# PSUM banks given out by number, the mixed key tile weighted in one pass, row sums over fewer slabs, shift copies on ScalarE

## The chip, the cores and the metric

The kernel runs on one core of a Trainium2 chip. The metric is device time in microseconds of one execution; the number for a kernel is the median of several executions.

## The reference

The input is x (4 sequences of 512 rows, 512 features) and a context of 1601 rows for each sequence, all fp32. Two parts follow each other.

The first is cross attention with 16 heads of 32 features on the layer norm of x. The first 257 context rows are an image part and the other 1344 a text part. Each has its own key and value weights; queries and keys are normalised by their root mean square and scaled. The queries attend to the text part and, in a softmax of its own, to the image part; the two results are added, projected and added to x.

```
q = rms_norm(linear(ln(x), q_w, q_b), norm_q_w)
k, v         = rms_norm(linear(ctx[:, 257:], k_w, k_b), norm_k_w), linear(ctx[:, 257:], v_w, v_b)
k_img, v_img = the same of ctx[:, :257] with the image weights
x = x + linear(attention(q, k, v) + attention(q, k_img, v_img), o_w, o_b)
```

The second is a mixture of experts on the layer norm of the new x (2048 tokens): a router picks 4 of 32 experts for each token out of its three best of 8 groups, each expert takes at most 80 tokens, and a shared gated layer is added.

## The kernel before

The work is put in order by hand: each engine executes its instructions in the order in which the Python program emits them, and waits are set by the use of tiles. A tile's buffer is written again once all uses of its last holder are done.

*Attention.* The outer loop runs over the 4 sequences `b`. For each, the keys of all heads are computed in four blocks (`keys`, L513 on; block 3 is the image part), with other work put between the chunks by the table `side` (L555) and the list after it. Then an inner loop runs over `c` = 0 to 3. One (b, c) is called a unit here: a group of 4 heads, 32 features each, so that a head `g` stands on partitions 32g to 32g+31. There are 16 units.

A unit walks over 13 key tiles `t` of 128 keys (`NKT`). The keys are laid out text first, so tile 10 (`MIX`) holds 64 text keys on the lower and 64 image keys on the upper partitions, and tile 12 has 65 keys. In each step t stand:

- `wave` (L312), only for c < 3: scores of queries against 512 keys for the *next* unit, four matmuls of 32 contraction rows side by side, and their maxima on VectorE (L336, L338, L331).
- `exps` (L364): for each of the 4 heads a bf16 matmul that puts in the negated maxima (L370, the shift, from `mT`), a matmul of keys by queries (L373) and the exponential on ScalarE (L374) into `pT` of that tile.
- `consume(t - 2)`: `weighted` (L376) multiplies the values with the exponentials of two steps ago into the bank `po`, four matmuls of 32 output columns each side by side (L379). Tile 10 ends the text sum and begins the image sum: its text half is weighted, `po` is copied out by ScalarE (`taken`, L604), a new `po` is taken, and its image half is weighted behind `exps` of that step.
- `added` (L381): the exponentials of the text tiles 0 to 9 are summed in `acc`, two adds of 128x1024 a tile, on GpSimd for c < 3 and on VectorE for c = 3 (L388).
- one value tile of the next unit (`value_tile`, L284), or for c = 3 a piece of the next sequence's queries, and other pieces, by `fill`.

The last two tiles and the row sums are put off: `pending` (L673) holds consume(11), consume(12) and `end`, which the next unit takes out at t = 0 (two) and t = 1 (L631, L646). Behind c = 3 the first is taken at once and the others in the next sequence's `side[(0, 0)]`, or, behind the last unit, in the loop over the first two shared projections at the end (L910). `end` calls `summed` (L390), which reduces four slabs over the partitions by matmuls with 0 and 1 (`sums`): `acc` and tiles 10, 11 and 12. `normalize` (L408) then sends the sums through DRAM to turn them about (den, reciprocal, `rb`), scales the two outputs on GpSimd (L423, L424) and adds them on VectorE into `aoT` (L425); `Later` counts the steps between these.

Before a unit, `split` (L340) forms the shifts of its maxima on VectorE as three bf16 terms, and `shifts` (L355) turns them by four transposes and copies the result to `mT` on VectorE (L361).

*Buffers.* The eight PSUM banks are a ring of 7 for all (`psum`) and one for `po`:

```
ring = pool("ring", 7, space=PSUM)
pso = pool("pso", 1, space=PSUM)
```

`pT` has 5 buffers, which also take the weights of the next sequence (wk, wki, wo, loaded by SP's queue) and the first tile of the shared layer (`first_xT`, L681). `po_s`, `den` and `sq_q` share 4 buffers.

*After attention* come the shared layer, with routing on VectorE between its projections, and the 32 experts, whose weights stream in.

Of the kernel before, what the change touches and what calls it, by code (L numbers as in the profile page):

```python
# [103 lines left out]
def body(ctx, tc, a, ident, mhalf, logits, x1_d, xw_d, xnT_d, den_d, rec_d, out):  # L104
# [10 lines left out]
    ring = pool("ring", 7, space=PSUM)  # L115
    pso = pool("pso", 1, space=PSUM)
    later = Later()

    def psum(dt=F32):

        shape = [P, 512] if dt is F32 else [P, NQ, P]
        return ring.tile(shape, dt, name="ps", tag="ring")
# [232 lines left out]
    def shifts(part):  # L355

        ps = psum(BF16)
        for qt in range(NQ):
            nc.tensor.transpose(ps[:, qt, :], part[:, qt, :], ident_b)
        mT = st.tile([P, L], BF16, name="mT", tag="mT", bufs=2)  # L360
        nc.vector.tensor_copy(mT, ps.rearrange("p t q -> p (t q)"))  # L361
        return mT
# [13 lines left out]
    def weighted(po, v, t, rows, pT, start, stop):  # L376
        for g in range(NG4):
            r = HD * g
            nc.tensor.matmul(po[r:r + HD, :], lhsT=v[rows, t, r:r + HD], rhs=pT[rows, g, :], start=start, stop=stop)  # L379

    def added(acc, pTs, t, idle):  # L381

        if t < 1 or t >= MIX:
            return
        for half in range(2):
            h = slice(2 * half, 2 * half + 2)
            engine = nc.vector if idle else nc.gpsimd
            engine.tensor_tensor(acc[:, h, :], pTs[0][:, h, :] if t == 1 else acc[:, h, :], pTs[t][:, h, :], ALU.add)  # L388

    def summed(acc, pTs):  # L390

        ps = psum()
        slabs = [(acc, 0)] + [(pTs[t], t) for t in range(MIX, NKT)]
        for j, (p, t) in enumerate(slabs):
            n = key_rows(t)
            for g in range(NG4):
                nc.tensor.matmul(
                    ps[g * HD:(g + 1) * HD, :],
                    lhsT=sums[:n, kind(t)].rearrange("p a b -> p (a b)"),
                    rhs=p[:n, g, :],  # L400
# [92 lines left out]
    for b in range(B):  # L493
# [52 lines left out]
        def due():  # L546
# [9 lines left out]
            (0, 0): [due, due, N("q")],  # L556
# [30 lines left out]
        for c in range(NC):  # L587
# [10 lines left out]
            def consume(t, c=c, v=v, pTs=pTs, outs=outs, pos=pos):  # L598

                n = key_rows(t)  # L600
                if t == 0:
                    pos.append(pso.tile([P, L], F32, name="po"))

                def taken():  # L604
                    o = held("po_s")
                    nc.scalar.copy(o, pos[-1])  # L606
                    outs.append(o)

                def text():
                    weighted(pos[0], v, t, slice(0, HALF), pTs[t], False, True)  # L610
                    taken()
                    pos.append(pso.tile([P, L], F32, name="po"))

                def image():
                    weighted(pos[1], v, t, slice(HALF, P), pTs[t], True, False)

                def all_():
                    weighted(pos[-1], v, t, slice(0, n), pTs[t], t == 0, t == NKT - 1)
                    if t == NKT - 1:
                        taken()  # L620

                return (text, image) if t == MIX else (all_, lambda: None)

            for t in range(NKT):
# [4 lines left out]
                if t == 0 and c:  # L629
                    mT = shifts(part)  # L630
                if t < 2 and pending:  # L631
                    pending.pop(0)()
                if t == 1:
                    g["acc"] = kv.tile([P, NG4, L], F32, name="acc")
                    if more:
                        v_next = kv.tile([P, NKT, P], F32, name="v", bufs=2)
                        fill = values(v_next, c + 1, cTs, ws)
                    elif b + 1 < B:
                        fill = work
                behind = consume(t - 2) if t > 1 else [lambda: None] * 2  # L640
                behind[0]()
                exps(c, t, qT, kT, mT, pT)
                if t:
                    added(g["acc"], pTs, t - 1, not more)
                behind[1]()
                if t == 0 and pending:  # L646
                    pending.pop(0)()
                if c == 0 and t < 3:
# [21 lines left out]
            def end(i=b * NC + c, c=c, aoT=aoT, outs=outs, acc=g["acc"], pTs=pTs):  # L670
# [349 lines left out]
```

## Time and profile before

| | |
|---|---|
| median of 3 runs | 1824.26 us (1822.17 to 1825.31) |
| profiled execution: time, span of its instructions | 1826.59 us, 1824.9 us |
| granted TensorE clock, mean | 0.987 |
| TensorE (PE) busy | 1737.6 us, 95% |
| VectorE (DVE), ScalarE (ACT), GpSimd (POOL) busy | 960.6, 614.8, 773.6 us |
| weighting matmuls L379, 1792 records | 238.7 us busy |
| exponentials L374, 832 | 429.4 us, 602 ns each |
| adds on GpSimd L388, 216 | 505.8 us, 2384 and 2353 ns each |
| adds on VectorE L388, 72 | 88.2 us, 1278 and 1221 ns each |
| matmuls of the row sums L397, 512 records | 64.0 us busy |

An fp32 matmul shows as two records, one for each pass; a bf16 matmul as one. Records of matmuls that run side by side overlap, and the end of a record is modelled, so the time that a group takes is read from its start to the next group's start. Times in the timelines are microseconds from the start of the span.

### The profile page before, as it was taken

What the parts mean: (1) busy time and instruction counts of PE and PEld (TensorE: products, weight loads), DVE (VectorE), ACT (ScalarE), POOL (GpSimd) and SP (SyncE); (2) the same over time, 40 slices, a digit from 0 to 9 for tenths busy, and PEclk for the clock granted to TensorE, in tenths of its full rate; (3) what the DMA queues carried; (4) which work ended last, traced back from release to release, by engine and by line L of the source; (5) the groups of instructions that cost most, each with busy time, mean ns of one, the idle gap of its engine ahead of it and who ended that gap; (6) DMA issues with size and microseconds to landing.
All of it is one profiled execution on the core that took longest, in us unless ns stands there. A gap on an engine that the chain in (4) does not pass through costs nothing. (4 is left out here: it accounts for less than half of the span.)

```text
span 1824.9 us, 29627 instructions
## 1 busy us (share of the span) xinstructions
PE 1737.6 (95%) x11985; PEld 906.5 (50%) x11985; DVE 960.6 (53%) x1881; ACT 614.8 (34%) x1324; POOL 773.6 (42%) x540
## 2 busy tenths in 40 slices
PE   4999999999999999999999999999999999999896
PEld 1564444446644444565444445644442454477664
DVE  2485557628555556475556547655465567611110
ACT  1124444621344446114444551144446110011111
POOL 1319558122468552326477323284591110123332
PEclk9999999999999999999999999999999999999898
DMA  6000000040100102120001030200012173279894
GB/s 217 1 1 1 19 5 28 22 146 29 65 1 20 31 2 105 62 68 27 11 10 31 14 143 18 98 13 14 2 36 82 65 252 104 65 250 296 267 294 118
DMA packets 68024, 138.41 MB, mean 76 GB/s; under 512 B 16048, under 2 KB 28464, under 8 KB 65584
## 3 DMA queue, kind: packets, MB, share of 16 engines
q1 hardware_dynamic: 62768, 125.70, 20.2%
q0 software_dynamic: 5120, 10.82, 2.9%
q8 instruction: 95, 1.56, 0.4%
q14 instruction: 41, 0.34, 0.1%
HBM read 113.68 MB, written 22.81 MB: 75 GB/s over the span
## 5 line engine op out<-in xcount | busy, mean ns | idle before, releaser
L374 ACT ACTIVATE pT<-ps 128x512 f32<-128x512 f32 (+1 forms) x832 | 429.4, 602 | 418.8 <-PE ps L373 407.8
L336 DVE TENSOR_REDUCE mx<-ps 128x1 f32<-128x512 f32 (+1 forms) x576 | 330.9, 616 | 294.6 <-PE ps L322 294.5
L388 POOL TENSOR_TENSOR acc<-acc,pT 128x1024 f32<-128x1024 f32 x192 | 449.8, 2384 | 10.6 <-ACT pT L374 10.6
L379 PE MATMUL po<-pT,v 128*32 128x512 f32 (+2 forms) x1792 | 238.7, 604 | 0.4 <-ACT po_s L606 0.4
L292 PEld LDWEIGHTS ps<-v_w,cT 128*128 128x128 f32 (+1 forms) x1408 | 170.5, 189 | 92.6 <-DVE mx L336 48.5
L373 PE MATMUL ps<-qT,kT 32*128 32x512 f32 (+1 forms) x1664 | 215.7, 589 | 0.0
L322 PE MATMUL ps<-kT,qT 32*128 32x512 f32 (+1 forms) x1536 | 202.5, 553 | 0.0
L292 PE MATMUL ps<-v_w,cT 128*128 128x128 f32 (+1 forms) x1408 | 196.8, 286 | 0.0
L232 PE MATMUL ps<-cT,wk 128*128 128x512 f32 (+1 forms) x384 | 153.1, 545 | 0.0
L310 DVE TENSOR_REDUCE mx<-ps 128x1 f32<-128x512 f32 (+2 forms) x256 | 128.3, 565 | 7.8 <-PE ps L307 7.8
L388 POOL TENSOR_TENSOR acc<-pT 128x1024 f32<-128x1024 f32 x24 | 56.0, 2353 | 168.0 <-ACT pT L374 168.0
L370 PEld LDWEIGHTS <-pick 32*128 32x128 bf16 (+1 forms) x832 | 22.2, 91 | 185.8 <-issue 162.5
L370 PE MATMUL ps<-mT,pick 32*128 32x512 bf16 (+1 forms) x832 | 87.8, 385 | 21.9 <-DVE mT L361 12.5
L894 POOL DMA_INDIRECT out<-y,tok x32 | 45.4, 1419 | 143.2 <-DMA out<-y,tok 85.0
L232 PEld LDWEIGHTS ps<-cT,wk 128*128 128x128 f32 x384 | 69.9, 190 | 69.4 <-issue 58.8
L379 PEld LDWEIGHTS po<-pT,v 128*32 128x32 f32 (+2 forms) x1792 | 35.4, 107 | 133.3 <-issue 112.7
L239 POOL TENSOR_TENSOR sq_k<-sq_k,sq 128x512 f32<-128x512 f32 (+2 forms) x48 | 49.5, 1031 | 121.7 <-ACT sq L236 121.7
L884 DVE TENSOR_TENSOR ehT<-ehT,ps 128x160 f32<-128x160 f32 x32 | 10.3, 321 | 164.3 <-ACT ehT L883 164.3
L300 ACT COPY v<-ps 128x128 f32<-128x128 f32 (+1 forms) x208 | 58.4, 289 | 108.3 <-PE ps L292 107.7
L322 PEld LDWEIGHTS ps<-kT,qT 32*128 32x128 f32 x1536 | 79.3, 185 | 28.8 <-issue 11.6
L239 POOL TENSOR_TENSOR sq_q<-sq_q,sq 128x128 f32<-128x128 f32 (+1 forms) x39 | 23.3, 605 | 162.5 <-ACT sq L236 162.4
L373 PEld LDWEIGHTS ps<-qT,kT 32*128 32x128 f32 (+1 forms) x1664 | 80.8, 180 | 16.8 <-issue 12.5
(173 smaller groups left out, 2142.3 us busy)
## 6 DMA issues: line engine op xcount, KB each, us to landing
W_gate<-in_W_gate SPq DMA_DIRECT2D x32, 512.0 KB, 5.8
W_up<-in_W_up SPq DMA_DIRECT2D x32, 512.0 KB, 7.0
W_down<-in_W_down SPq DMA_DIRECT2D x32, 512.0 KB, 4.9
xt<-in_x SPq DMA_DIRECT2D x32, 256.0 KB, 2.6
cT<-in_ctxT SPq DMA_DIRECT2D x8, 1024.0 KB, 9.0
rb<-rec_d SPq DMA_DIRECT2D x64, 128.0 KB, 2.7
wk<-in_k_w SPq DMA_DIRECT2D x4, 1024.0 KB
wki<-in_k_img_w SPq DMA_DIRECT2D x4, 1024.0 KB, 9.2
```

Of the source, the lines that this page charges most:

```text
L232: nc.tensor.matmul(ps[:, :n], lhsT=wt[:, k, c * P:(c + 1) * P], rhs=xT[:, k, to], start=k == 0, stop=k == NC - 1)
L239: nc.gpsimd.tensor_tensor(sq[:, to], sq[:, to], s, ALU.add)
L292: nc.tensor.matmul(ps[lo:hi, :], lhsT=cTs[bl][:, k, at:at + hi - lo], rhs=ws[bl == NB - 1][:, k, c * P:(c + 1) * P], start=k == 0, stop=k ...
L300: nc.scalar.copy(v[:n, t, :], ps[:n])
L310: nc.vector.tensor_reduce(mx[:, qt, g, bl:bl + 1], ps[:, :n], AX.X, ALU.max, negate=True)
L322: nc.tensor.matmul(ps[:, j * n:(j + 1) * n], lhsT=qT[r:r + HD, c, q * P:(q + 1) * P], rhs=kT[r:r + HD, c, k0:k0 + n], start=True, stop=True,)
L336: nc.vector.tensor_reduce(mx[:, qt, g, i:i + 1], ps[:, :m], AX.X, ALU.max, negate=True)
L370: nc.tensor.matmul(ps[:n], lhsT=pick[r:r + HD, kind(t), :n], rhs=mT[r:r + HD, :], start=True, stop=False)
L373: nc.tensor.matmul(ps[:n], lhsT=kT[r:r + HD, c, t * P:t * P + n], rhs=qT[r:r + HD, c, :], start=False, stop=True)
L374: nc.scalar.activation(pT[:n, g, :], ps[:n], AF.Exp)
L379: nc.tensor.matmul(po[r:r + HD, :], lhsT=v[rows, t, r:r + HD], rhs=pT[rows, g, :], start=start, stop=stop)
L388: engine.tensor_tensor(acc[:, h, :], pTs[0][:, h, :] if t == 1 else acc[:, h, :], pTs[t][:, h, :], ALU.add)
```

## The change

The two PSUM pools become one of eight single buffers, named by bank number. A list gives the banks out in turn; `kept` takes one out of the list for `po`, and `taken` puts it back after the copy. At tile 10 both halves are now weighted in one loop over the heads, text and image alternating, each into its own bank, ahead of `exps` of that step.

In c < 3 tile 12 is added to tile 11 (its 65 partitions) by GpSimd after consume(11), so that `summed` has three slabs: `acc`, tile 11 and tile 10. In c = 3 VectorE also adds the text half of tile 10 to `acc` and its image half to tile 11, so that there are two. `end` is taken at t = 2 instead of t = 1, `acc` is begun at t = 2 after it, and the first value tile of t = 1 is put ahead of `exps`. For c > 0 the shift copy is done by ScalarE. At the start of a sequence the pending tasks are taken one step apart, and likewise at the first two shared projections.

```diff
-    ring = pool("ring", 7, space=PSUM)
-    pso = pool("pso", 1, space=PSUM)
+    ring = pool("ring", 1, space=PSUM)
+    banks = list(range(8))
...
-        return ring.tile(shape, dt, name="ps", tag="ring")
+        banks.append(banks.pop(0))
+        return ring.tile(shape, dt, name="ps", tag=f"bank{banks[-1]}")
+
+    def kept():
+
+        n = banks.pop(0)
+        return ring.tile([P, 512], F32, name="po", tag=f"bank{n}"), n
...
-    def shifts(part):
+    def shifts(part, copy=nc.vector.tensor_copy):
...
-        nc.vector.tensor_copy(mT, ps.rearrange("p t q -> p (t q)"))
+        copy(mT, ps.rearrange("p t q -> p (t q)"))
...
-    def weighted(po, v, t, rows, pT, start, stop):
+    def weighted(v, t, pT, *to):
+
         for g in range(NG4):
             r = HD * g
-            nc.tensor.matmul(po[r:r + HD, :], lhsT=v[rows, t, r:r + HD], rhs=pT[rows, g, :], start=start, stop=stop)
-
-    def added(acc, pTs, t, idle):
-
-        if t < 1 or t >= MIX:
-            return
+            for po, rows, start, stop in to:
+                nc.tensor.matmul(
+                    po[r:r + HD, :], lhsT=v[rows, t, r:r + HD], rhs=pT[rows, g, :], start=start, stop=stop
+                )
+
+    def added(to, pT, rows, idle):
+
         for half in range(2):
             h = slice(2 * half, 2 * half + 2)
-            engine = nc.vector if idle else nc.gpsimd
-            engine.tensor_tensor(acc[:, h, :], pTs[0][:, h, :] if t == 1 else acc[:, h, :], pTs[t][:, h, :], ALU.add)
+            (nc.vector if idle else nc.gpsimd).tensor_tensor(to[rows, h, :], to[rows, h, :], pT[rows, h, :], ALU.add)
+
+    def begun(pTs, idle):
+
+        acc = kv.tile([P, NG4, L], F32, name="acc")
+        for half in range(2):
+            h = slice(2 * half, 2 * half + 2)
+            (nc.vector if idle else nc.gpsimd).tensor_tensor(acc[:, h, :], pTs[0][:, h, :], pTs[1][:, h, :], ALU.add)
+        return acc
...
-            (0, 0): [due, due, N("q")],
+            (0, 0): [due, N("q")],
+            (0, 1): [due],
...
+            def taken(pos=pos, outs=outs):
+                po, n = pos.pop(0)
+                o = held("po_s")
+                nc.scalar.copy(o, po)
+                banks.append(n)
+                outs.append(o)
+
+            def consume(t, v=v, pTs=pTs, pos=pos, taken=taken):
+
+                if t in (0, MIX):
+                    pos.append(kept())
+                if t == MIX:
+                    weighted(
+                        v, t, pTs[t], (pos[0][0], slice(0, HALF), False, True), (pos[1][0], slice(HALF, P), True, False)
+                    )
+                else:
+                    weighted(v, t, pTs[t], (pos[0][0], slice(0, key_rows(t)), t == 0, t == NKT - 1))
+                if t in (MIX, NKT - 1):
                     taken()
...
                 if t == 0 and c:
-                    mT = shifts(part)
-                if t < 2 and pending:
+                    mT = shifts(part, nc.scalar.copy)
+                if t in (0, 2) and pending:
                     pending.pop(0)()
                 if t == 1:
-                    g["acc"] = kv.tile([P, NG4, L], F32, name="acc")
                     if more:
                         v_next = kv.tile([P, NKT, P], F32, name="v", bufs=2)
                         fill = values(v_next, c + 1, cTs, ws)
+                        fill[0]()
+                        done = 1
...
-                behind = consume(t - 2) if t > 1 else [lambda: None] * 2
-                behind[0]()
+                if t > 1:
+                    consume(t - 2)
                 exps(c, t, qT, kT, mT, pT)
-                if t:
-                    added(g["acc"], pTs, t - 1, not more)
-                behind[1]()
                 if t == 0 and pending:
                     pending.pop(0)()
+                if t == 2:
+                    g["acc"] = begun(pTs, not more)
+                elif 2 < t <= MIX:
+                    added(g["acc"], pTs[t - 1], slice(0, P), not more)
+                elif t == NKT - 1 and not more:
+                    added(g["acc"], pTs[MIX], slice(0, HALF), True)
...
+            def image(consume=consume, pTs=pTs, idle=not more):
+
+                consume(NKT - 2)
+                added(pTs[NKT - 2], pTs[NKT - 1], slice(0, key_rows(NKT - 1)), idle)
+                if idle:
+                    added(pTs[NKT - 2], pTs[MIX], slice(HALF, P), idle)
+
+            def end(i=b * NC + c, c=c, aoT=aoT, outs=outs, acc=g["acc"], pTs=pTs, idle=not more):
+                slabs = [(acc, 0), (pTs[NKT - 2], 2)] + ([] if idle else [(pTs[MIX], 1)])
+                normalize(i, c, aoT, *outs, summed(slabs))
+
+            pending += [image, partial(consume, NKT - 1), end]
...
         u()
-        while pending:
+        if pending:
             pending.pop(0)()
         later.step()
```

More of the change, by code (lines that the diff above doesn't have):

```diff
@@ L374, in exps, with summed @@
             nc.scalar.activation(pT[:n, g, :], ps[:n], AF.Exp)
-    def weighted(po, v, t, rows, pT, start, stop):
+    def weighted(v, t, pT, *to):
         for g in range(NG4):
             r = HD * g
-            nc.tensor.matmul(po[r:r + HD, :], lhsT=v[rows, t, r:r + HD], rhs=pT[rows, g, :], start=start, stop=stop)
-    def added(acc, pTs, t, idle):
-        if t < 1 or t >= MIX:
-            return
+            for po, rows, start, stop in to:
[3 more added lines that the diff above has]
+    def added(to, pT, rows, idle):
         for half in range(2):
             h = slice(2 * half, 2 * half + 2)
-            engine = nc.vector if idle else nc.gpsimd
-            engine.tensor_tensor(acc[:, h, :], pTs[0][:, h, :] if t == 1 else acc[:, h, :], pTs[t][:, h, :], ALU.add)
-    def summed(acc, pTs):
+            (nc.vector if idle else nc.gpsimd).tensor_tensor(to[rows, h, :], to[rows, h, :], pT[rows, h, :], ALU.add)
[5 more added lines that the diff above has]
+        return acc
+    def summed(slabs):
         ps = psum()
-        slabs = [(acc, 0)] + [(pTs[t], t) for t in range(MIX, NKT)]
-        for j, (p, t) in enumerate(slabs):
-            n = key_rows(t)
+        for j, (p, k) in enumerate(slabs):
             for g in range(NG4):
@@ L398, in summed @@
                     ps[g * HD:(g + 1) * HD, :],
-                    lhsT=sums[:n, kind(t)].rearrange("p a b -> p (a b)"),
-                    rhs=p[:n, g, :],
+                    lhsT=sums[:, k].rearrange("p a b -> p (a b)"),
+                    rhs=p[:, g, :],
                     start=j == 0,
@@ L596, in body @@
             pTs, outs, pos, g = [], [], [], {}
[L598 to L610, printed above, removed]
-                    taken()
[L612 to L622, printed above, removed]
+            def taken(pos=pos, outs=outs):
[14 more added lines that the diff above has]
+                if t in (MIX, NKT - 1):
+                    taken()
             for t in range(NKT):
@@ L668, in body @@
                         turn[t // 3][1]()
-            def end(i=b * NC + c, c=c, aoT=aoT, outs=outs, acc=g["acc"], pTs=pTs):
-                normalize(i, c, aoT, outs[0], outs[1], summed(acc, pTs))
-            pending += [lambda consume=consume, t=t: consume(t)[0]() for t in (NKT - 2, NKT - 1)] + [end]
+            def image(consume=consume, pTs=pTs, idle=not more):
[7 more added lines that the diff above has]
+            pending += [image, partial(consume, NKT - 1), end]
             if more:
```

## The prediction, made before the changed kernel had run

> **What bounds the kernel now.** I read the page's engine rows and slices first, then the timeline of TensorE across a boundary of two head groups, then the list of its waits in the same windows.
>
> ```profile
> PE 1737.6 (95%) x11985; PEld 906.5 (50%) x11985; DVE 960.6 (53%) x1881; ACT 614.8 (34%) x1324; POOL 773.6 (42%) x540
> PE   4999999999999999999999999999999999999896
> ```
>
> TensorE is full in all slices but the first and those of the experts at the end. Attention runs from about 130 to 1415 us, and there nearly every matmul removed is time removed. The chain of waits holds only the tail's scatter, so I work from timelines. The end of c=0 and the start of c=1 in sequence b=1 (start, length, engine, line; in brackets the idle time before):
>
> ```profile
> 534.86 1.06 PE L379 MATMUL po<-pT,v 64*32 64x512 f32 x8
> 535.85 0.41 PE L370 MATMUL ps<-mT,pick 32*65 32x512 bf16 x4
> 536.09 1.03 PE L373 MATMUL ps<-qT,kT 32*65 32x512 f32 x8
> 537.05 1.06 PE L379 MATMUL po<-pT,v 64*32 64x512 f32 x8
> 538.04 1.09 PE L292 MATMUL ps<-v_img_w,cT 128*65 128x128 f32 x8
> 539.06 1.14 PE L322 MATMUL ps<-kT,qT 32*128 32x512 f32 x8
> 540.13 0.40 PE L359 MATMUL ps<-ident_b,parts 128*128 128x128 bf16 x4
> 540.46 1.06 PE L379 MATMUL po<-pT,v 128*32 128x512 f32 x8
> 543.09 0.40 PE L370 MATMUL ps<-mT,pick 32*128 32x512 bf16 x4 [1.56 <-DVE mT L361]
> ```
>
> Rows overlap at their ends, so starts are the clock. The two 64-row groups of the mixed tile (534.86, 537.05) take 0.99 us each to the next start. The second follows the scores with no gap, so the wait for the one `po` bank, 13.5 us in the list of waits, lies under other work. At 543.09 TensorE stood still for 1.56 us: the shift copy waits on VectorE behind four maxima.
>
> ```profile
> 546.34 1.06 PE L397 MATMUL ps<-acc,sums 128*32 128x512 f32 x8
> 547.22 2.76 PE L397 MATMUL ps<-pT,sums 128*32 128x512 f32 x24
> 549.91 0.40 PE L370 MATMUL ps<-mT,pick 32*128 32x512 bf16 x4
> ```
>
> Four slabs of row sums: 547.22 to 549.91 is three, about 0.865 us each (0.43 us a pass, two passes). And one stall in c=2:
>
> ```profile
> 635.56 2.46 DVE L425 SCALAR_TENSOR_TENSOR aoT<-po_s,v_b 128x512 f32<-128x512 f32 x1
> 637.94 2.57 DVE L221 TENSOR_SCALAR xl<-xt,mv,rstd 128x512 f32<-128x512 f32 x1
> 641.16 0.37 PE L370 MATMUL ps<-mT,pick 32*128 32x512 bf16 x1 [2.25 <-DVE mx L336]
> ```
>
> Two VectorE operations that take 0.74 and 0.44 us elsewhere take 2.5 each, back to back, while GpSimd adds; the maxima then come late and banks are not free. The step from the shift matmuls at 638.53 to the next at 647.48 is 8.95 us against 5.01 for its like (624.46 to 629.47), partly because matmuls after the gap are slower: 3.94 us lost. It occurs three times (gaps near 288, 639 and 990 us).
>
> **What the skill says.** "TensorE: Matmul & The Clock Gate", Packing small matmuls, says that tiles of different row and column groups run together and that both kinds compose. The trace agrees for four row tiles (L373) and four column tiles (L379), 7 ns apart in start; eight of 64x32 it doesn't show. "SBUF — State Buffer", Who interferes with whom, says that VectorE with two SBUF inputs, or in a two-port mode, and GpSimd block each other, and tensor_reduce never does: the 2.5 us rows agree, and the maxima keep their 0.6 us. The clock page's account that idleness throttles TensorE agrees with the values group after that gap, 1.91 us instead of 1.16.
>
> **The change, part by part** (16 units: 4 sequences of c=0..3).
>
> *Mixed tile.* The image group moves beside the text group. If eight tiles run as four do, one 0.99 us is saved per unit. But in c=0 and 1 (8 units) the next wave then comes 0.99 us sooner, and its fourth bank waits for the second exp of tile 12: exps start 1.12 us after the scores and take 0.52 each, so it is free at 2.2 against a wave at 2.0; cost 0.24. Leaves 8 x 0.75 = 6.0. At the ends of c=3 for b<3, 3 x 0.99 = 3.0. At c=2's end the gain meets the shift copy, next.
>
> *Shift copy to ScalarE*, 12 copies. This form isn't in the trace; the nearest rows are ScalarE's fp32 copies of 128x512, 0.59 to 0.62 us, and VectorE's own copy, 0.42. I take 0.6; up to 1.0 would hide in c=1 and 2. In c=1 and 2 ScalarE is through with tile 12 before the transposes end, and the copy hides under consume(11), 1.0 us: 8 x 1.56 = 12.5. In c=3 there is no wave; VectorE was free and nothing waited. Now the copy queues behind tile 12's exps, the copy of xl and the value copy: these end 3.8 us after the scores began (674.85), so it ends at 4.4, where TensorE wants it at 3.65. That costs 0.8 of c=2's 0.99 (leaves 0.2, x4 with b=3, where no xl copy stands but TensorE is sooner too). Total for the mixed tile, this charged: 6.0 + 3.0 + 0.8 = 9.8.
>
> *Row sums.* c<3 drops one slab, c=3 two: 12 x 0.865 + 4 x 1.73 = 17.3. The one at the start of b=3's c=3 counts below, so 16.4. For it GpSimd adds tile 12 onto tile 11, 2 x 2.36 us (L388's row) in t=0, after consume(11) and tile 12's exps. Behind it queue only inv_sqrt and the next `acc`. The sums now stand in t=2: between lie exps, consume(12), a wave, two values, exps and a wave, about 8 us, so it hides; in c=3 about 5 us, and its slab comes after `acc`'s 0.87. Without that cover up to 4.7 us per unit would show. Per unit GpSimd rises from about 45 to 50 us, under some 62. In c=3 VectorE makes six adds of 1.2 us at the end instead, under keys (3.6 us a chunk) and consume(12); ready about 5 us after consume(11), needed after 9. The weights loaded into these buffers (wo on SP's queue) wait for the last add rather than for the sums, about as late as now.
>
> *`end` one step later.* It moves den's two DMAs, rec's store and rb's four loads on SP, the reciprocal, GpSimd's two scalings and aoT by a step; in c=2 the SP ones fall behind an x load of 0.37 us. rb is issued by 560.4 and used at 567.0, so there is slack. In c=2 aoT now follows t=6 and xl stays at t=5: two blocked operations no longer meet. One alone makes the maxima at most about 1 us late, with 0.5 slack. Unknown in size: 0 if they still meet, 11.8 (3 x 3.94) if not; single blocked ones leave no gap now, so I take 10. The first value matmul takes the place of the sums in t=1: no cost, as none is added.
>
> *Banks by number.* po waits cost nothing now, so nothing is gained; six are left for a moment at the mixed tile, but the bank taken held the third exp of tile 11, done 0.6 us earlier. Zero; up to 0.5 x 16 = 8 lost if not.
>
> *Last unit* (b=3, c=3). VectorE's adds bound it: the xT load is issued when its buffer's add is done.
>
> ```profile
> 1403.68 0.61 SPq L681 DMA_DIRECT2D xT<-xnT_d  x1
> 1409.73 2.80 PE L226 MATMUL ps<-xT,shared_gate 128*128 128x512 f32 x4 [3.02 <-DMA xT<-xnT_d]
> ```
>
> Here the matmuls saved are lost in that wait. But exps(1) comes before the sums, so VectorE begins at about 1379.0 rather than 1381.3 in before's clock: 2.2 saved. Taking one pending task per shared unit moves the sums behind one more projection, at no cost.
>
> Sum: 9.8 + 12.5 + 16.4 + 10 + 2.2 = 50.9 us. The profiled execution took 1826.6 (span 1824.9), 2.3 above the median of the runs, 1824.3; I take the difference from the median: 1773.4.
>
> **Rivals.**
> (1) *The eight tiles do not overlap* beyond the old pace: two groups back to back keep 2.0 us less a switch of modes (0.12). Then 0.87 x 16 goes less the 4 us charged for coming sooner, about 10: 1783; if the double block stays too, 1793. For it: no such group in the trace. Against: both halves of the array's tiling do overlap.
> (2) *GpSimd becomes the wait.* If its pair comes late, by a backlog or VectorE's blocking, the sums in t=2 stall TensorE with everything behind them. At 3 us in each of 12 units it gives back 36: 1810. Against it: GpSimd idles 22.5 us before `acc` (552.48) and has finished by then.
> (3) *Slower: tiles sharing a column group go one after another.* Text and image are interleaved by g, so if each of the 16 passes of 0.43 us ran alone, the mixed tile would take 6.9 instead of 2.0 us: +4.9 x 16 = 78, against 41 saved by the other parts: about 1861. It decides from about 4.6 us per mixed tile up (2.0 + 41/16). For it: they use the same output columns at once. Against: the four row tiles of L373 do so as well, and start 4 ns apart.
> (4) *The change does less than it says*, because banks by number wait in other places: 8 back, 1782.
>
> **Numbers.** Forecast as summed, 0.64; rivals 1 and 4, 0.22; rival 2, 0.07; rival 3 or another loss of that size, 0.05; no difference, 0.02. A measurement tells about 0.2% (3.6 us) from none. Faster 0.93, same 0.02, slower 0.05. The range goes down to 1761: the double block wholly gone (1.8 more), no wait of the wave (1.9) nor of the shift copy in c=3 (3.2), and the 3.0 us gap ahead of the shared gate gone with its slow matmuls (5.37 instead of 3.7 us, 1.7), 11.6 in all. Up it goes to 1802, which takes in rivals 1 and 4 together.
>
> **What would show it.** Right: one L379-like group of 16 records of 64x32 per unit spanning about 1.1 us; no gap of 1.56 before the shift matmuls in c=1, 2, a new one near 0.8 in c=3; 352 records of the sums' matmuls instead of 512; the gaps near 288, 639, 990 gone. Wrong: that group at 2 us or more, a wait of the sums on GpSimd, or a gap before the wave of t=0 well over 0.24.

## The result and the profile after

| | before | after |
|---|---|---|
| median | 1824.78 us (1822.17 to 1829.25, 4 runs) | 1803.19 us (1797.12 to 1812.46, 4 runs) |
| ratio after / before | | 0.9884, interval 0.9837 to 0.993 |
| profiled execution: time, span | 1826.59, 1824.9 us | 1803.62, 1801.9 us |
| granted TensorE clock | 0.987 | 0.984 |

By these runs the kernel became 1.2% faster; two later sets of runs of the same kernel gave 2.4% and 1.7% (experiment 1). 1803.19 lies just above the end of the range (1802) and 29.8 us over the forecast of 1773.4. The page of after, its engine row and the row of the one new kind of work (tile 12 added to tile 11 on GpSimd: busy us and mean ns, then GpSimd's idle time before it):

```profile
PE 1709.7 (95%) x11825; PEld 899.0 (50%) x11825; DVE 1002.6 (56%) x1893; ACT 621.7 (35%) x1336; POOL 830.4 (46%) x564
L395 POOL TENSOR_TENSOR pT<-pT 65x1024 f32<-65x1024 f32 x24 | 56.0, 2352 | 109.1 <-PE po L387 89.4
```

TensorE has 160 records less, all of them row sums (352 of L410 for 512 of L397), and is still full. GpSimd carries 57 us more, the 56.0 of the second row, and in the 24 places it was idle for 109.1 us in all until its input came. Of VectorE's work only maxima stand beside these additions, so they hold nothing up. VectorE's busy time rose by 42 us. Its 24 more additions in c=3, less twelve copies, make some 24 of that; two single rows of 9.44 us, one of them shown below, make some 14 of the rest.

The end of c=0 and the start of c=1 in sequence b=1, the timeline of TensorE in after (start, length, engine, line; in brackets the idle time before):

```profile
530.75 1.09 PE L387 MATMUL po<-pT,v 64*32 64x512 f32 x16
531.77 0.41 PE L376 MATMUL ps<-mT,pick 32*65 32x512 bf16 x4
...
535.31 0.40 PE L365 MATMUL ps<-ident_b,parts 128*128 128x128 bf16 x4
535.64 1.06 PE L387 MATMUL po<-pT,v 128*32 128x512 f32 x8
536.64 0.39 PE L376 MATMUL ps<-mT,pick 32*128 32x512 bf16 x4
...
544.32 1.06 PE L410 MATMUL ps<-acc,sums 128*32 128x512 f32 x8
545.20 1.90 PE L410 MATMUL ps<-pT,sums 128*32 128x512 f32 x16
546.92 1.04 PE L387 MATMUL po<-pT,v 128*32 128x512 f32 x8
```

All that the forecast said of this stretch is there. The mixed tile is one group of 16 records that takes 1.02 us to the next start. The shift matmuls at 536.64 carry no bracket: the stall of 1.56 us is gone. The sums after `acc` take 545.20 to 546.92, two slabs where there were three.

What the forecast did not say stands in c=1 of b=0, in the timeline of all engines, of which these are the rows of one stall:

```profile
216.91 1.27 POOL L437 TENSOR_TENSOR po_s<-po_s,rb 128x512 f32<-128x512 f32 x1
218.13 9.27 POOL L395 TENSOR_TENSOR acc<-acc,pT 128x1024 f32<-128x1024 f32 x4
218.51 9.44 DVE L438 SCALAR_TENSOR_TENSOR aoT<-po_s,v_b 128x512 f32<-128x512 f32 x1
228.60 0.58 PE L376 MATMUL ps<-mT,pick 32*128 32x512 bf16 x1 [6.48 <-DVE mx L342]
232.00 4.67 POOL L395 TENSOR_TENSOR acc<-acc,pT 128x1024 f32<-128x1024 f32 x2 [4.59 <-ACT pT L380]
```

`aoT`'s addition on VectorE takes 9.44 us where it takes 0.74 alone and took at most 2.47 in before. It lasts through four additions on GpSimd and ends when GpSimd has no more that is ready: its next one, at 232.00, waits 4.59 us for an exponential. The maxima stand behind `aoT` on VectorE, no bank comes free, and TensorE waits 6.48 us; the matmuls after that run slower too (the scores in 2.28 us instead of 1.03): the granted clock is 0.50 from 228.6 to 231 and back at 1.00 only from 234 on. That step takes 12.94 us where its like takes 4.53. The same happens in c=1 of b=3, with the same gap of 6.48 us; there the clock was 0.50 for longer (1257 to 1263), and the step takes 13.76 us. I call this a shut-out. Together the two cost 8.4 + 9.2 = 17.6 us. In b=1, `aoT` began as long after a GpSimd addition (0.37 us) and was let in at the next one, after 2.52 us.

And c=2, where the forecast counted the double stall as gone (the same views, sequence b=1). `xl` is the next sequence's x tile, normalised on VectorE with its mean and with `rstd`, the inverse of its deviation, which GpSimd makes:

```profile
631.74 2.83 DVE L438 SCALAR_TENSOR_TENSOR aoT<-po_s,v_b 128x512 f32<-128x512 f32 x1 [1.63 <-POOL po_s L437]
635.22 0.37 PE L376 MATMUL ps<-mT,pick 32*128 32x512 bf16 x1 [1.20 <-DVE mx L342]
642.35 2.57 DVE L227 TENSOR_SCALAR xl<-xt,mv,rstd 128x512 f32<-128x512 f32 x1 [0.98 <-POOL rstd L214]
645.57 0.37 PE L376 MATMUL ps<-mT,pick 32*128 32x512 bf16 x1 [1.02 <-DVE mx L342]
```

One gap of 2.25 us became two of 1.2 and 1.0, and each of the two VectorE operations now has idle time before it, in which VectorE waits for GpSimd. Part of what this row saves is the clock's: behind each of the three gaps of 2.25 us in before the granted clock fell to half (0.50 from 643 to 645), and in after it stays at 1.00 through this stretch (631 to 650).

To see where the sum went I cut each trace at the first shift matmuls of every unit and add up the units of one kind. The values are us saved against the trace of before; the last column is explained with the experiments. The shared gate, or gate for short, is the first matmul of the shared layer.

| stretch | forecast | after | a second run of after | late_moments_early |
|---|---|---|---|---|
| before the first unit | 0 | 1.4 | 1.3 | -0.1 |
| c=0, four units | 9.2 | 10.3 | 10.3 | 10.3 |
| c=1, four units | 12.7 | **-4.8** | 12.8 | 12.8 |
| c=2, b<3, three units | 13.2 | **5.8** | 5.5 | 11.4 |
| c=2, b=3 | 1.1 | 1.5 | 1.5 | 1.5 |
| c=3 and the next keys, three | 10.8 | 10.5 | 10.5 | 10.1 |
| last unit to the shared gate | 2.2 | 1.4 | 1.3 | 2.4 |
| from there to the end | 1.7 | -3.0 | -1.4 | 2.4 |
| sum | 50.9 | 23.0 | 41.9 | 50.8 |

The forecast column is its own terms by place (c=0: 1.56 + 0.75; c=1: the same and 0.865 for a slab; c=2: 0.865 + 0.2 + 3.33; c=3: 0.865 + 1.73 + 0.99). It is met within 1.4 us in every row but two of the attention's and the last one.

### The profile page after: what moved, and what is told of

It reads as the page before. It is cut to its first block, busy times and chain, and to the rows that moved or that the text cites. A ratio compares the mean times of both kernels' runs of the same rounds, so it can differ in the third digit from the quotient of the medians.

```text
span 1801.9 us, 29352 instructions
## 1 busy us (share of the span) xinstructions
PE 1709.7 (95%) x11825; PEld 899.0 (50%) x11825; DVE 1002.6 (56%) x1893; ACT 621.7 (35%) x1336; POOL 830.4 (46%) x564
## 5 line engine op out<-in xcount | busy, mean ns | idle before, releaser
L387 PE MATMUL po<-pT,v 128*32 128x512 f32 (+2 forms) x1792 | 221.9, 603 | 0.0
L395 POOL TENSOR_TENSOR pT<-pT 65x1024 f32<-65x1024 f32 x24 | 56.0, 2352 | 109.1 <-PE po L387 89.4
L376 PEld LDWEIGHTS <-pick 32*128 32x128 bf16 (+1 forms) x832 | 21.8, 91 | 167.4 <-issue 164.1
L904 DVE TENSOR_TENSOR ehT<-ehT,ps 128x160 f32<-128x160 f32 x32 | 10.3, 321 | 164.1 <-ACT ehT L903 164.1
## 6 DMA issues: line engine op xcount, KB each, us to landing
wki<-in_k_img_w SPq DMA_DIRECT2D x4, 1024.0 KB, 10.2
```

What stands on the lines that cost most here:

```text
L376: nc.tensor.matmul(ps[:n], lhsT=pick[r:r + HD, kind(t), :n], rhs=mT[r:r + HD, :], start=True, stop=False)
L395: (nc.vector if idle else nc.gpsimd).tensor_tensor(to[rows, h, :], to[rows, h, :], pT[rows, h, :], ALU.add)
```

## The experiments

Theory: the parts are worth what the forecast says; what is missing are shut-outs of `aoT`, and stalls in c=2 that come from GpSimd's queue. Rivals: the mixed tile or the slabs are worth less than thought; GpSimd is the bound; the interleaving matters. All edits are to the changed kernel unless said. Each ratio is to the kernel before, run on the same chip.

**1. The changed kernel again**, unedited, on two chips.

> The changed kernel as it is, profiled again. Starved VectorE: which of the 16 aoT adds is shut out for some 9.4 us is a matter of timing within a few ns, so the number of them (two in the first profile, in b=0 and b=3) may differ, each worth 8.4 to 9.2 us of TensorE, and runs spread over steps of about that size (about 1787 with none, 1796 with one, 1804 with two, 1812 with three). Fixed pattern: the same two units again and runs within 3 us of 1803.

> The changed kernel as it is, a third time, beside the next ones. By the theory of the shut-out VectorE: about 1782 plus 8.4 to 9.2 us for each aoT add that waits 9.4 us; the profile shows how many.

Measured: after_again 1782.03 us, ratio 0.9762 (0.9739 to 0.9785); after_third 1791.42 us, 0.9827 (0.98 to 0.9854), single runs from 1785.45 to 1799.71. In both profiled executions no `aoT` row is over 2.84 us, and c=1 saves 12.8 us as forecast. So shut-outs come in some executions and not in others, and the kernel's time moves by some 8 to 9 us with each. That the other runs of the first result held between one and three of them each (1797.12 to 1812.46 us) is argued from their times, since only one of them has a trace.

**2. `aoT` moved off VectorE, or to where it stood.**

```diff
 # aot_off_dve
-later.after(1, lambda: nc.vector.scalar_tensor_tensor(aoT[:, c, :], po_t, v_b[:, c:c + 1], po_i, ALU.add, ALU.add))
+nc.gpsimd.tensor_tensor(po_t, po_t, po_i, ALU.add)
+later.after(1, lambda: nc.scalar.activation(aoT[:, c, :], po_t, AF.Identity, bias=v_b[:, c:c + 1]))
 # scale_1
-            later.after(2, scale)
+            later.after(1, scale)
```

> The changed kernel, with the sum of the two scaled outputs made on GpSimd (one more add of 128x512, 1.28 us a unit) and the bias put in by ScalarE, so VectorE has no aoT add. Starved VectorE: both gaps of 6.48 us are gone with their slow matmuls (17.6), and in c=2 the gap of 1.2 us behind aoT: 1803 - 18 - 4 = about 1781, and runs within 3 us of each other. GpSimd's backlog as the cause instead: it gets 1.28 us more to do per unit, the gaps stay or grow: 1803 to 1815.

> The changed kernel with the scaling one step earlier, so that aoT stands at the end of t=5 again as in the kernel before, the rest as changed. Starved VectorE as a matter of phase: no wait of 9 us in c=1 (it meets the adds at another point, about 2.0 us as before), but in c=2 aoT and xl meet at t=5 again: 3 x about 3 us lost there; 1803 - 17.6 + 6 = about 1792. If the later place of aoT has nothing to do with it: two waits of 9.4 us remain, 1803 or more.

Measured: aot_off_dve 1803.87 us, 0.9871 (0.9849 to 0.9894), slower than the changed kernel on the same chip. One more addition per unit in GpSimd's queue makes `rstd` late; gaps of 3.2 to 3.4 us stand ahead of shift matmuls in c=2, and in c=3 ScalarE waits for `aoT`'s input with the exponentials behind it (gaps of 1.02 us, and one of 5.02 in the last unit). So it missed its 1781: the shut-outs are gone with `aoT` off VectorE, but the new work on GpSimd and ScalarE costs 21.8 us against the changed kernel on that chip. scale_1 1788.54 us, 0.9788 (0.9766 to 0.981), near its 1792: without a shut-out in its profile, but `aoT` meets `xl` in c=2 again and gaps of up to 2.46 us are back. Since the changed kernel's own second and third profiles have no shut-out either, scale_1 alone doesn't show that the old place is free of them.

**3. Shorter additions.** GpSimd's additions in four pieces of 128x512 instead of two of 128x1024.

```diff
 # quarters (the same in begun); before_quarters: this edit in the kernel before
-        for half in range(2):
-            h = slice(2 * half, 2 * half + 2)
+        for h in range(2 if idle else NG4):
+            h = slice(2 * h, 2 * h + 2) if idle else h
 # quarters_late: quarters, and in normalize
-                later.after(1, lambda: nc.vector.scalar_tensor_tensor(
+                later.after(7 if i + 1 < B * NC else 1, lambda: nc.vector.scalar_tensor_tensor(
 # quarters_gaps: quarters, and after each second piece
+            if not idle and h % 2:
+                nc.gpsimd.tensor_scalar(breath, mhalf[:, 0:1], 1.0, 0.0, ALU.mult, ALU.add)
```

> The changed kernel with GpSimd's adds of exponentials cut into four of 128x512 per tile instead of two of 128x1024 (VectorE's as they were). If the port changes hands at the next end of a GpSimd instruction: no VectorE wait above 1.3 + 0.7 = 2 us, gaps of 6.48 gone, single gaps of c=2 smaller; each cut costs GpSimd about 0.1 us a tile: about 1783 to 1787. If VectorE is shut out until GpSimd has nothing ready: waits of up to 9 us remain as often or more often, 1800 or more.

> Adds of 128x512 as in quarters, and aoT's addition moved from step 7 of the next unit to the end of step 12. Theory (the five waits of 10.28 us in quarters are aoT's own, shut out by GpSimd's back-to-back adds, and each cost a step of 14.7 to 15.6 us where 4.53 is the usual): 5 x 10.6 = 53 us come back, and with them also some 1 to 2 us lost elsewhere, so about 1787 against 1836 for quarters; no VectorE row of aoT over 2.9 us. Rival A (smaller adds make GpSimd itself too slow, and the lost time is GpSimd's): it stays over 1815. Rival B (the shut-out takes whatever VectorE operation with two ports meets a run of adds): the xl rows of c=2 are shut out in its place, three of about 10 us, about 1815.

> The additions on GpSimd in pieces of 128x512, as in quarters, and after each second piece a tensor_scalar of 128x1 on GpSimd that nobody reads. Theory (VectorE's aoT is let in when GpSimd turns to an instruction that doesn't hold the port; in quarters' c=2, where rstd's small operations stand between the adds, none was shut out in b<3): no aoT over about 3.5 us, the five waits of 10.28 us gone, about 1836 - 5 x 8 = 1796, less a few us for the longer queue. Rival (only a GpSimd that has run out of ready work lets it in): five waits of 10 us or more stay, about 1836 or slower.

> The kernel before with GpSimd's additions in pieces of 128x512; nothing of the change is in it. Theory (the shut-out comes from where the change puts aoT, one step later, when GpSimd has fallen behind): no aoT row over 2.5 us, and the time within 6 us of before, about 1826. Rival (any aoT that meets a run of small adds is shut out, wherever it stands): five waits of about 10 us in c=1 of each b and c=2 of b=3, about 1824 + 5 x 9 = 1870.

quarters: 1836.48 us, 1.0056 (1.0034 to 1.0077), slower than before. Shorter pieces were to let VectorE in sooner; instead it was shut out in every c=1 and in c=2 of b=3, for 10.28 us each. The timeline of one of the five:

```profile
573.16 1.29 POOL L437 TENSOR_TENSOR po_s<-po_s,rb 128x512 f32<-128x512 f32 x1
574.38 9.83 POOL L395 TENSOR_TENSOR acc<-acc,pT 128x512 f32<-128x512 f32 x8
574.48 10.28 DVE L438 SCALAR_TENSOR_TENSOR aoT<-po_s,v_b 128x512 f32<-128x512 f32 x1 [0.54 <-POOL po_s L437]
585.42 0.58 PE L376 MATMUL ps<-mT,pick 32*128 32x512 bf16 x1 [7.94 <-DVE mx L342]
588.32 2.49 POOL L395 TENSOR_TENSOR acc<-acc,pT 128x512 f32<-128x512 f32 x2 [4.11 <-ACT pT L380]
```

Eight additions pass, and again the end is where GpSimd runs dry (4.11 us of idle time before the next). quarters_late puts `aoT` at the end of step 12, past the additions: 1785.86 us, 0.9793 (0.9769 to 0.9817), as its theory had it (1787). The 2.6% between the two ratios, some 48 us, are what moving `aoT` alone gains. `xl`, which meets the same additions, got in after 1.5 us at most.

quarters_gaps sets a tiny operation between pairs of pieces: 1799.54 us, 0.9865 (0.9843 to 0.9887), near the 1796 of its theory. The timeline:

```profile
564.32 2.50 POOL L395 TENSOR_TENSOR acc<-acc,pT 128x512 f32<-128x512 f32 x2
564.40 2.97 DVE L442 SCALAR_TENSOR_TENSOR aoT<-po_s,v_b 128x512 f32<-128x512 f32 x1 [1.49 <-POOL po_s L441]
566.79 0.63 POOL L397 TENSOR_SCALAR breath<-mhalf 128x1 f32<-128x1 f32 x1
```

In all five places `aoT` now takes 2.97 us and ends with the tiny operation, which takes 0.63 us there and about 0.2 elsewhere, as if VectorE ran in that time. So a GpSimd instruction of another kind ends a shut-out; it need not be idle. Between additions of one kind VectorE is let in at some boundaries (c=2 of quarters, 1.74 us, after one piece, well ahead of the `rstd` operations that the theory named) and not at others. What decides is open: the time from the start of an addition to `aoT`'s own start doesn't (0.07 us in quarters' c=1 and c=2 alike; 0.38 us in after with both outcomes).

before_quarters: 1817.57 us, 0.9963 (0.995 to 0.9976). No `aoT` row is over 1.71 us; in the kernel before it is not shut out even by short pieces, where quarters has five shut-outs. That fits the theory that the change's later place for it matters. It doesn't show it, because the two runs differ by the whole change, and GpSimd's backlog at that point is hardly another: in c=1 of b=1 its pairs of additions begin 1.8 to 2.8 us behind their exponentials in before, once the scalings are in, and 2.1 to 2.9 us in after. The time missed its expectation on the good side: the double stall of c=2 shrank, from a step of 8.92 to one of 5.71, because each blocked operation waits for 1.3 us of addition and not for 2.4, and the clock doesn't fall there.

**4. `aoT` at the end of step 12** (the edit of `later.after(7 ...)` above, with additions of 128x1024). late_halves_apart has also the mixed tile's text loop and image loop one after the other, in place of interleaved.

> The changed kernel with aoT six steps later (end of t=12 instead of t=6, save in the last unit), where GpSimd has worked off its adds; nothing else differs, GpSimd's load included. Shut-out VectorE: no wait of 9 us and no gap of 1.2 us behind aoT in c=2 (3 x 1.5), and in the last unit VectorE no longer stands 2.4 us for the scaling: 1782 - 4.4 - 2.4 = about 1775, and the runs close together. Load of GpSimd as the cause: as many and as long gaps as in the changed kernel beside it, same time.

> As the one with aoT late, but the two halves of tile 10 weighted in two loops, text then image, at the same place. If the eight 64x32 tiles of the change run side by side: about 0.87 us more per unit at tile 10, less what c=2 and 3 hide: 16 x 0.87 = 14, less 4: about +10. If interleaving gave nothing: same time, and the group of 16 records starts as two groups 0.87 us apart in both.

Measured: aot_late 1789.13 us, 0.9803 (0.9781 to 0.9825); late_halves_apart 1787.2, 0.9789 (0.9768 to 0.981). No `aoT` row of aot_late is over 0.79 us, but the time is not the 1775 hoped for: the stall of c=2 moved to `xl`. The order of issue is worth nothing. In both traces the first passes of all eight tiles start 7 ns apart, and 0.45 us after the first of them the eight second ones; c=0's unit is 60.56 us in both (b=1 to 3). Rival 3 of the prediction is out, and two loops would have done.

**5. Parts undone.** late_vec_shift and late_four_slabs undo one part each in aot_late; late_early_apart undoes the mixed tile in late_moments_early (number 6): text half before step 12's scores, image half behind its exps, as before.

```diff
 # late_vec_shift
-mT = shifts(part, nc.scalar.copy)
+mT = shifts(part)
 # late_four_slabs (and no additions to or of tiles 10 to 12)
-slabs = [(acc, 0), (pTs[NKT - 2], 2)] + ([] if idle else [(pTs[MIX], 1)])
+slabs = [(acc, 0)] + [(pTs[t], t) for t in range(MIX, NKT)]
 # late_early_apart
-    weighted(v, t, pTs[t], (pos[0][0], slice(0, HALF), False, True), (pos[1][0], slice(HALF, P), True, False))
+    weighted(v, t, pTs[t], (pos[0][0], slice(0, HALF), False, True))
 ...
 exps(c, t, qT, kT, mT, pT)
+if t == MIX + 2:
+    weighted(v, MIX, pTs[MIX], (pos[0][0], slice(HALF, P), True, False))
```

> As the one with aoT late, but the shift copy on VectorE as in the kernel before. By the prediction's step: gaps of 1.56 us or more return before the shift matmuls of c=1 and 2 (8 of them, now with consume(11) alone to cover, 12.5 us), the 0.6 us gap at c=3's start goes (about 3 x 0.6): about +10.5. Rival: the queue on ScalarE costs as much as it saves: within 3 us.

> aoT's addition at the end of step 12 and the row sums again over four slabs of 128, 128, 128 and 65 rows, with no additions of tiles 11 to 13 on GpSimd or VectorE. Theory (a slab costs TensorE 0.865 us and hides nowhere; GpSimd's extra adds are free): 12 x 0.865 + 4 x 1.73 - 0.865 = 16.4 us slower than the same kernel with folded slabs (1789): about 1805. Rival (GpSimd's two extra adds per unit feed the waits for scaling and rstd in c=2, so that dropping them repairs some of those): the step at t=9 of c=2 falls from 7.3 to 8.8 towards 5.0 and the kernel is at about 1797 or below.

> late_moments_early with the mixed tile's two halves apart again: the text half before step 12's scores and exps, the image half behind them, as in the kernel before; everything else stays. Theory (the second group of 64x32 tiles costs TensorE its own 0.99 us unless it runs beside the first): between 9.8, the forecast's term, and 16 x 0.99 = 15.8 us slower, gate at about 1371 to 1377, and c=0's unit from 60.56 to 61.3 or more. Rival (the image half fills a time in which TensorE waits for a bank anyway): within 3 us of late_moments_early.

(In the second text the tiles are counted from 1.) What undoing a part cost, in us, from the traces up to the shared gate, with the time of the runs behind it:

| | c=0 | c=1 | c=2, b<3 | c=2, b=3 | c=3, b<3 | last | time, ratio |
|---|---|---|---|---|---|---|---|
| late_vec_shift | 5.5 | 5.0 | -3.0 | -0.4 | -0.8 | 0.4 | 1792.88, 0.9822 (0.9801 to 0.9843) |
| late_four_slabs | 0 | 3.4 | 0.2 | 1.0 | 6.3 | 0.3 | 1798.28, 0.9853 (0.9826 to 0.988) |
| late_early_apart | 2.9 | 3.2 | 0.1 | 0.4 | 3.1 | 0.3 | 1786.94, 0.979 (0.9775 to 0.9805) |

The mixed tile is worth 10.0 us where the forecast had 9.8, and with the same shape: 0.72 us a unit in c=0 (0.75 forecast), 0.04 in c=2 (0.2), 1.02 in c=3 (0.99). In c=2 the likeness is luck: the forecast lost the gain to the shift copy, and in these two kernels no gap stands before the shift matmuls of c=3 in b<3. TensorE waits at the transposes ahead of them instead, 1.64 us with one pass and 0.63 with the halves apart (number 7). The shift copies are worth 10.5 us in c=0 and 1, for 12.5; with VectorE's copy the gap there is 1.31 us now. In c=3 the ScalarE copy leaves its gap of 0.63 us; the 3.0 of c=2 holds that and the stall's own spread. (Behind the same gap of 2.0 us, the slow step of aot_late is 7.31 us in b=1, where the clock stays at 1.00, and 8.76 in b=0, where it falls to 0.57.) With all columns the copies are worth 6.7 us, and the medians of the two runs differ by 3.75 us, which is within their intervals: as a gain of the whole kernel this part isn't shown. A slab is worth 0.85 us in c=1 (0.865), 1.0 in c=2 of b=3, 2.1 in c=3 with the next keys (2.6), and next to nothing in c=2 of b<3 and in the last unit, where the matmuls saved fall into a wait. So late_four_slabs came out at 1798 and not at 1805. Its gap of 2.0 us in c=2 stays, though GpSimd has no tile 12 to add: that extra work is not what stalls c=2.

**6. The stall of c=2.**

```diff
 # late_moments: aot_late, and the moments of an x tile ahead of the step's additions
+if c == NC - 2 and b + 1 < B and t % 3 == 1 and t < 3 * NQ:
+    turn[t // 3][0]()
 if t == 2:
     g["acc"] = begun(pTs, not more)
 # late_moments_early: the same one step earlier, at t in (1, 3, 6, 9), x tiles loaded at t in (0, 2, 5, 8)
```

> aoT's addition at the end of step 12, and in c=2 the moments of an x tile (bn_stats, bn_aggr and GpSimd's two small operations for rstd) issued ahead of that step's additions on GpSimd, not behind them. Theory (what is left of the stall in c=2 is xl waiting for rstd in GpSimd's queue): in step 9 of c=2 the gap of 1.02 to 2.06 ahead of the shift matmuls goes and the step falls from 7.3 to 8.8 us to about 5.0, so 3 x 3 = 9 us come back: about 1779. Rival (xl meets the adds wherever it stands and stays blocked for 2.5 us; the stall is the block, not the wait): within 3 us of 1788, the slow step stays.

> As late_moments, and the x tiles of c=2 are loaded one step earlier (t = 0, 2, 5, 8) with the moments at t = 1, 3, 6, 9 ahead of that step's additions, so that rstd stands right behind the scaling in GpSimd's queue and ahead of the additions that hid it. Theory (xl waits for rstd, which waits for GpSimd's backlog): VectorE's idle time of 2.1 us ahead of xl at t=8 goes, the step of 8.7 us falls to 6.5 or less, and TensorE starts the shared gate at about 1363 instead of 1370.8: about 1776. Rival (xl is blocked by the adds for 2.5 us in any place and that alone makes the maxima late): the step stays at 7.2 or more, gate at 1369 or later, about 1783.

aot_late, the timeline of c=2 in b=1:

```profile
627.54 9.29 POOL L395 TENSOR_TENSOR acc<-acc,pT 128x1024 f32<-128x1024 f32 x4
637.19 0.55 POOL L214 TENSOR_TENSOR rstd<-rstd,mhalf 128x1 f32<-128x1 f32 x1
637.78 2.56 DVE L227 TENSOR_SCALAR xl<-xt,mv,rstd 128x512 f32<-128x512 f32 x1 [2.08 <-POOL rstd L214]
640.99 0.37 PE L376 MATMUL ps<-mT,pick 32*128 32x512 bf16 x1 [2.02 <-DVE mx L342]
```

GpSimd adds 2 x 2.35 = 4.7 us in a step that lasts 4.5 to 5.0. The scalings (2 x 1.27) put it behind, and it doesn't catch up: four additions stand before `rstd`, so VectorE waits 2.08 us for it with nothing to do, then `xl` meets the next addition and takes 2.56. late_moments moved `rstd` past one pair and gained nothing certain: 1782.89 us, 0.9789 (0.9759 to 0.982), gate at 1370.8 us as before, gap 2.05. late_moments_early moved it past one more:

```profile
623.55 1.27 POOL L437 TENSOR_TENSOR po_s<-po_s,rb 128x512 f32<-128x512 f32 x1
625.18 0.55 POOL L214 TENSOR_TENSOR rstd<-rstd,mhalf 128x1 f32<-128x1 f32 x1
625.70 14.12 POOL L395 TENSOR_TENSOR acc<-acc,pT 128x1024 f32<-128x1024 f32 x6
630.22 2.75 DVE L227 TENSOR_SCALAR xl<-xt,mv,rstd 128x512 f32<-128x512 f32 x1
```

`rstd` stands right behind the scaling, `xl` has no idle time before it, and although it is blocked as long as ever (2.75 us) TensorE has no gap left in that step: it fell from 8.7 to 5.33 us, the gate to 1361.4. The time is 1776.27 us, 0.9737 (0.9716 to 0.9758). The wait was the stall, not the block. (A block at the end of c=2 still costs something: number 7.)

**7. Towards a better one.** late_moments_c3 and late_early_c3 give c=3's shift copy back to VectorE; best has pieces of 128x512 as well.

```diff
-mT = shifts(part, nc.scalar.copy)
+mT = shifts(part, nc.scalar.copy if more else nc.vector.tensor_copy)
```

> The kernel with aoT at step 12 and the moments ahead of the adds, and in c=3 alone the shift copy again on VectorE. Theory (in c=3 no wave of maxima stands ahead of the copy on VectorE, while on ScalarE it queues behind the last exps: the gap of 0.63 us is the change's own loss there): 4 x 0.6 = 2.5 us faster than the one without this edit, about 1776, and no gap of 0.6 ahead of the first shift matmuls of c=3. Rival (the gap turns into a wait for a bank or for the exps): the same as without it.

> aoT at the end of step 12, additions in pieces of 128x512, the moments as in late_moments_early, and c=3's shift copy on VectorE. Theory (a blocked VectorE operation waits at most for the piece under way, 1.3 us instead of 2.4; in quarters_late xl took 1.47 us where 128x1024 adds made it 2.56): no step of c=2 over 6 us, the shared gate at about 1359 and the time about 1773. Rival (shorter pieces make GpSimd fall behind, 4 x 1.26 = 5.04 us for a step of 4.53, and rstd comes late by that): a gap of 2 us or more stays in c=2, about 1783.

> late_moments_early with c=3's shift copy on VectorE, ScalarE's kept in c=1 and 2. Theory (on ScalarE the copy queues behind tile 12's exps, and the gap of 0.6 us ahead of c=3's first shift matmuls is that): the gap goes in all four c=3, gate at about 1361.4 - 4 x 0.6 = 1359, time about 1774. Rival (VectorE's copy there queues behind aoT, which is added at the end of step 12 and then takes up to 2.7 us beside the adds): the gap grows to 1 us or more, gate at 1361 or later.

late_moments_c3: 1787.74 us, 0.9799 (0.9774 to 0.9824), not told apart from late_moments. best: 1783.52, 0.9775 (0.9752 to 0.9797), a miss: steps 5 to 9 of c=2 take 5.02 us at most, but at the end of c=2 a gap of 3.3 us stands where `split` on VectorE runs beside a GpSimd that is still adding. late_early_c3: 1775.3, 0.9722 (0.9705 to 0.974), not told apart from late_moments_early. Its edit had nothing to remove in b<3. The gap there stands at the transposes, ahead of the shift copy, and it is the same in both kernels (two rows of late_moments_early, b=1, then two of late_early_c3, b=0):

```profile
648.04 2.70 DVE L438 SCALAR_TENSOR_TENSOR aoT<-po_s,v_b 128x512 f32<-128x512 f32 x1
652.18 0.40 PE L365 MATMUL ps<-ident_b,parts 128*128 128x128 bf16 x4 [1.64 <-DVE parts L357]
310.79 2.66 DVE L438 SCALAR_TENSOR_TENSOR aoT<-po_s,v_b 128x512 f32<-128x512 f32 x1
314.88 0.40 PE L365 MATMUL ps<-ident_b,parts 128*128 128x128 bf16 x4 [1.59 <-DVE parts L357]
```

The rival named the right thing in the way, `aoT`, held for 2.7 us beside the additions. But what waits behind it is `split` (`parts`), not the copy. It costs late_moments_early 1.6 us in each of three sequences.

## Why the prediction was wrong, point by point

**What held.** The mixed tile (9.8 forecast, 10.0 by undoing it), with the wave's wait in c=0 and 1 and the loss in c=3: the gap there, `[0.63 <-ACT mT L367]` in the trace of after, was put at 0.8. The shift copies in c=0 and 1: the gaps of 1.56 are gone, and undoing them there costs 10.5 us where the forecast had 12.5. The row sums outside c=2 and the last unit. Banks by number cost nothing that shows, though no run undoes them alone: c=0 and, where no shut-out stands, c=1 save what was forecast or more. Rivals 1 and 3 are refuted by the mixed tile's 1.02 us, rival 4 by this. Rival 2 had the right engine and the wrong wait: not the sums wait for GpSimd, but `aoT` and `xl`. One reading was off, without consequence: the four row tiles of L373 start 2 to 4 ns apart in the trace of before, and only the column tiles 7.

**The step that failed is "`end` one step later".** It said of c=2: "two blocked operations no longer meet. One alone makes the maxima at most about 1 us late, with 0.5 slack". It failed twice.

First, by size: one alone can be held for 9.44 us. The forecast took the rows of some 2.5 us in before as the size of the block. In the shut-outs seen, what ends it is that GpSimd runs out of ready additions or turns to another kind of instruction. The page "SBUF — State Buffer" of the Trainium skill, Summary: rules for kernel authors, says that the second to issue "fully blocks until the first finishes"; these runs disagree: behind the addition under way, three further ones of 128x1024 went first, and seven of 128x512. The shut-outs came in c=1, where the forecast looked for no effect; that the later place of `aoT` brings it on is argued, not shown (number 3). This took 17.6 us of the profiled execution; it is the -4.8 in the table in place of 12.7. It was not priced as a case, so the range didn't reach it. That the median fell outside the range at all is partly the luck of the draw: the other two medians of the same kernel, 1782.03 and 1791.42, lie inside. The second failure stands in all three traces.

Second, by mechanism: in c=2 the term of 10 us came from `aoT` and `xl` meeting each other. Apart, they still stalled, because both wait for results out of GpSimd's queue, which is later now: `aoT` waits for the scalings, `xl` for `rstd` behind the additions. c=2 saved 5.8 us and not 13.2 (5.5 and 4.0 in the other two traces); the term is about 2.6 instead of 10. The forecast saw that GpSimd rises "from about 45 to 50 us, under some 62" in a unit, but the unit's average hides that in steps 3 to 10 its additions take 4.7 us of 4.5 to 5.0, with the scalings on top. The test is late_moments_early: with `aoT` out of the way and `rstd` early c=2 saves 11.4 us, and the whole sum is 50.8 us against the 50.9 of the forecast (1776.27 us by the median of its runs). That they agree to 0.1 us is luck, since the last row moves by several us from trace to trace; up to the gate it is 48.4 against 49.2. So the sum was about right for a kernel whose GpSimd queue was put in order; the changed kernel isn't that one.

**The last unit**: 1.4 for 2.2. TensorE's gap ahead of the shared gate grew from 3.02 to 3.81 us. **From there to the end** the trace of after is 3.0 us longer than that of before, without a cause in the change that I found: with the same code there, the stretch from the first expert's gate to the end took 215.6 to 223.8 us in the other traces, and 219.5 and 222.8 in these two, so the difference lies within that spread.

**Left open**: what decides at a boundary between two additions whether VectorE is let in, and so how many shut-outs an execution of the changed kernel has, and why the kernel before has none.

## What to carry to other kernels

When a two-input VectorE operation is moved, look at what GpSimd has ready at its new place, not at how long such an operation was blocked at the old one: it can be held through the whole run of ready GpSimd work. Compare a helper engine's work with the length of the *step* in which it is due and not with the unit's total, since an engine at 46% of the span can be behind for six steps on end (2.5 to 5.0 us in c=2 of aot_late, b=1), and everything small that passes through its queue (a scaling, an `rstd`) is late by that backlog. When a stall is counted as gone because two causes no longer meet, ask of each what it waits for by itself.

## What the runs showed of the hardware that was not expected

- VectorE's addition with two SBUF inputs was shut out through 4 GpSimd additions of 128x1024 (9.44 us) and 8 of 128x512 (10.28 us). With the long ones this came twice in one profile of the kernel and not at all in two others. Halving the pieces made it worse by 54 us against the same kernel on the same chip (1836.48 to 1782.03). A GpSimd tensor_scalar of 128x1 between pairs ended it after 2.97 us, five times of five.
- `xl`, a tensor_scalar with one SBUF input, was held by the same additions for at most 2.8 us (128x1024) or 1.6 us (128x512), never for a run of them.
- Eight 64x32 fp32 tiles, two in each column group, take 1.02 us to the next start, as four do (0.99), interleaved or one loop after the other.
- Whether TensorE's granted clock fell went with how long it stood. Behind the three gaps of 2.25 us in before it fell to half for about 3.4 us; behind the eight of 1.56 us there, and the six of 1.0 to 1.2 us in c=2 of after, it didn't. Behind the three of 2.0 us in aot_late it fell twice, and behind the two of 6.48 us for 6.8 and 10.2 us.
